# A state-space vision network on one core: a depthwise 13 x 13 convolution that takes 16 channels at a time and does its 13th kernel column as sixteen 32x32 products

## The chip, the cores and the metric

The kernel runs on one core of one Trainium2 chip. The metric is device time in microseconds: the median of three runs before the change is 6902.47 us (6889.23 to 6907.38). The profile is one further execution.

The engines are named as the profile names them: PE is TensorE's matmul side and PEld its weight loads, DVE is VectorE, ACT is ScalarE, POOL is GpSimd, SP is SyncE, which here only issues DMAs. ACT and POOL issue DMAs as well; an issued DMA then runs on 16 DMA engines that all queues share.

## What is computed

Eight images of 384 channels and 32 x 32 points go through four layers: two state-space blocks (the second with an attention gate and an MLP), a sum of seven depthwise convolutions with batch norms, and a pointwise convolution followed by a depthwise one with GELU. The change concerns the last two. Cut to what matters:

```python
def _L2_conv_ref(x, w_lk, w_b0, ..., bn_gamma, bn_beta, bn_mean, bn_var):
    dilates = (1, 1, 2, 3, 4, 5)
    out = bn_eval(dwconv(x, w_lk, 1), bn_gamma[0], ...)          # 13 x 13
    for i, (w, r) in enumerate(zip(branch_ws, dilates)):         # 5, 7, 7, 3, 3, 3
        out = out + bn_eval(dwconv(x, w, r), bn_gamma[i + 1], ...)
    return out

def _L3_conv_ref(x, pw_w, ..., dwk_w, ..., dw1_w, ...):
    x_pw = bn(einsum('bchw,oc->bohw', x, pw_w), ...) + x
    out = bn(dwconv(x_pw, dwk_w), ...)                           # 13 x 13
    out = out + bn(x_pw * dw1_w.reshape(1, -1, 1, 1), ...)
    return gelu(out, approximate=False)
```

All the branches of one layer together are one depthwise convolution with a 13 x 13 kernel per channel, and that is how the kernel does them. All arithmetic is in float32.

## The kernel before

**Order.** `network` first runs `layers`, the two state-space blocks and the MLP, up to about 6347 us of the span. There the order of each engine's instructions is written out by hand: a `Plan` has numbered slots, and every step is put into one. Then come `Depthwise.run` on `x3` (called run 1 here), `Pointwise.run`, and `Depthwise.run` on `x5` (run 2). These three have no order written by hand; the framework puts the instructions of each engine in a queue, and each queue runs in order.

**The kernel tables.** `prepare` is a generator whose pieces are put into consecutive slots near the beginning, from slot -50 on. It folds the batch norms, and for each of the two convolutions (`k2`, `k3`) and each of three chunks of 128 channels it loads the branch kernels (line 190, POOL's queue, seven loads for `k2` and one for `k3`), sums them on DVE into one 13 x 13 kernel (198 or 202 and 204), zeroes a row buffer of 1024 values (206), copies the kernel into it in four pieces (210), and stores it to `k_rows` in DRAM with one DMA from POOL's queue (212), 4096 contiguous bytes for each partition. In the table the 13 columns of a kernel stand as 4 steps `j` (`KP = 4`) by 4 shifts `s`, column 4 j + s, so three of the sixteen places are empty; the 13 rows stand in a strip of `HK = 64` rows of zeros. A small pair of steps before it (140, 145) writes 384 biases out in 4-byte pieces and reads them back.

**The depthwise step.** One step `g` of 48 takes 8 channels, as two sets `a` of four channels `q`. A channel's images stand in `xp` with 32 image rows on 32 partitions, and four copies of them, shifted by 0, 1, 2 and 3 columns, stand in the four groups of 32 partitions. Two DMAs from POOL's queue load the images (`images`, line 984), one for the first and one for the second set, and four DVE copies make the shifts (999 to 1001): two of 32 partitions by 1212 values, two of 64 by 1208. `kernels` (970) loads the tables into `wt`: a band matrix for each column, made by reading the strip of zeros at 32 offsets, 512 contiguous bytes per partition and channel, in four DMAs of 128 KB, three from SP's queue and one from ACT's. `early` loads the first ten steps' tables ahead, from POOL's queue, while `layers` is still at its last MLPs.

A product (1008) has 128 rows of contraction, 32 output rows of one channel and 256 columns (8 images x 32). For one set it runs over `j` and then over the four `q`, which lie in different groups of 32 output columns of the array. The set's 128 x 256 outputs fill one PSUM tile; ACT adds the bias, with GELU in run 2 (1013), and issues the store (1014). The store of run 1 has 1024 contiguous bytes for each partition, that of run 2 eight pieces of 128 bytes.

**Buffers.** `xps` has 4, `wts` 11, `o` 4, and the PSUM pool 4 tiles of one bank. A `past` tile of 16100 values per partition and one of four PSUM banks lie ahead of the convolution's buffers: there are the buffers that `layers` uses to its end (`fh`, `rows_out`, the PSUM tiles `mm` and `f`), and what lies behind can be filled earlier. `Pointwise` has its buffers behind those of the convolution, and shares its PSUM pool.

Of the kernel before, what the change touches and what calls it, by code (L numbers as in the profile page):

```python
# [17 lines left out]
B = 8  # L18
# [20 lines left out]
PAST = 16100  # L39
# [27 lines left out]
class Plan:  # L67
# [3 lines left out]
    def __init__(self):  # L71
        self.slots = {}
# [4 lines left out]
    def run(self, slot):  # L77
        for fs in self.slots.pop(slot, ()):
            for f in fs:
                f()  # L80
# [30 lines left out]
def prepare(nc, k, vec, a, dram, tile, mm, got):  # L111
# [69 lines left out]
    for name in ("k2", "k3"):  # L181
        got[name] = dram.tile([C, 4, HK, KP], F32, name=f"{name}_rows")
        for c in range(KC):
            room, used[0] = tile("fh"), 0
# [20 lines left out]
            rows = tile("hc").rearrange("p q t -> p (q t)")[:, 0 : 4 * HK * KP]  # L205
            nc.vector.memset(rows, 0.0)
            rows = rows.rearrange("p (s r j) -> p s r j", s=4, j=KP)
            for s in range(4):
                n = (KS - s + 3) // 4
                nc.vector.tensor_copy(rows[:, s, low : low + KS, 0:n], t[:, s::4].rearrange("p j r -> p r j"))  # L210
            yield
            nc.gpsimd.dma_start(got[name][c * P : (c + 1) * P], rows)
# [730 lines left out]
class Depthwise:  # L943

    N2 = NG // 2
    NB, AHEAD = 4, 3
    NK, EARLY = 11, 10

    def __init__(self, tc, st):
        nc = self.nc = tc.nc
        self.keep = st.enter_context(tc.tile_pool(name="d_keep", bufs=1, reuse_waits="tile"))
        self.work = st.enter_context(tc.tile_pool(name="d_work", bufs=4, reuse_waits="tile"))
        self.psum = st.enter_context(tc.tile_pool(name="d_ps", bufs=4, space=PSUM, reuse_waits="tile"))
        self.wts = [self.keep.tile([P, 8, HW, KP], F32, name=f"wt{i}") for i in range(self.NK)]  # L960
        self.xps = [self.keep.tile([P, 8, B * WIDE + 2 * PAD], F32, name=f"xp{i}") for i in range(self.NB)]
        for t in self.xps:
            nc.gpsimd.memset(t, 0.0)

    def kernels(self, g, table, queues):
        wt = self.wts[g % self.NK]
        for s, queue in enumerate(queues):
            at = table.offset + (32 * g + s) * HK * KP
            windows = bass.AP(table.tensor, at, [[KP, HW], [4 * HK * KP, 8], [1, HW * KP]])
            queue.dma_start(wt[HW * s : HW * (s + 1)].rearrange("p q r j -> p q (r j)"), windows)  # L970
# [14 lines left out]

    def run(self, src, table, bias, func, store):
        nc = self.nc
        n = B * WIDE
        for g in range(self.AHEAD):
            self.images(g, src)  # L990
        for g in range(self.N2):
            wt, xp = self.wts[g % self.NK], self.xps[g % self.NB]
            if g + self.AHEAD < self.N2:
                self.images(g + self.AHEAD, src)
            if g + self.EARLY < self.N2:
                self.kernels(g + self.EARLY, table, (nc.sync, nc.scalar, nc.sync, nc.sync))
            for h in range(2):
                low, q = 2 * HW * h, slice(4 * h, 4 * h + 4)
                nc.vector.tensor_copy(xp[low + HW : low + 2 * HW, q, 0 : n - 1], xp[low : low + HW, q, 1:n])
            nc.vector.tensor_copy(xp[2 * HW :, 0:4, 0 : n - 2], xp[: 2 * HW, 0:4, 2:n])  # L1000
            nc.vector.tensor_copy(xp[: 2 * HW, 4:8, 2:n], xp[2 * HW :, 4:8, 0 : n - 2])
            for a in range(2):
                ps = self.psum.tile([P, T], F32, tag="ps", name="ps")
                for j in range(KP):
                    x = xp[:, :, 4 * j : 4 * j + n].rearrange("p q (b c) -> p q b c", c=WIDE)
                    for q in range(4):
                        c = 4 * a + q
                        nc.tensor.matmul(  # L1008
                            ps[HW * q : HW * (q + 1), : B * HW], wt[:, c, :, j], x[:, c, :, 0:HW],
                            start=j == 0, stop=j == KP - 1,  # L1010
                        )
                o = self.work.tile([P, B, HW], F32, tag="o", name="o")
                nc.scalar.activation(o, ps[:, : B * HW], func, bias=bias[:, 2 * g + a : 2 * g + a + 1])  # L1013
                nc.scalar.dma_start(store(2 * g + a), o)


class Pointwise:
# [4 lines left out]
    def __init__(self, tc, st, psum, w):  # L1022
        nc = self.nc = tc.nc
        keep = st.enter_context(tc.tile_pool(name="q_w", bufs=1, reuse_waits="tile"))
        self.work = st.enter_context(tc.tile_pool(name="q_work", bufs=3, reuse_waits="tile"))
        self.psum = psum
# [31 lines left out]
def network(ctx: ExitStack, tc: tile.TileContext, a: dict, out: bass.AP):  # L1058
# [36 lines left out]
    with ExitStack() as st:  # L1095

        past = st.enter_context(tc.tile_pool(name="past", bufs=1, reuse_waits="tile"))
        past.tile([P, PAST], F32, name="past")
        past_ps = st.enter_context(tc.tile_pool(name="past_ps", bufs=1, space=PSUM, reuse_waits="tile"))
        past_ps.tile([P, 4 * T], F32, name="past_ps")  # L1100
# [3 lines left out]
        point = Pointwise(tc, st, conv.psum, a["pw"])  # L1104
# [121 lines left out]
```

## Time and profile before

| What | us |
|---|---|
| Median of three runs | 6902.47 |
| Profiled execution: span from the first to the last instruction | 6870.5 |
| First matmul of run 1 | 6349.3 |
| First matmul of run 2 | 6671.5 |
| PE busy in the span | 5851.1 |
| DVE busy | 5755.9 |
| POOL busy | 5285.7 |
| ACT busy | 4475.3 |
| DVE copies of line 999, 192 of them | 153.6 |
| DVE copies of lines 1000 and 1001, 192 of them | 152.8 |
| ACT activations of line 1013, 192 of them | 91.0 |

The span is that of the profiled execution, and the difference to the median is what lies around it. A matmul of the program in float32 shows as two instructions. Busy time of a pipelined PE counts an instruction from its start to its modelled end, so four that overlap are counted once. The DMA share of a stretch can be over 1, as packets of several queues overlap on an engine.

This is the DMA view of the tables, images and stores (output and input, queue, number, size of each, median us to landing):

```profile
wt<-k_rows SPq DMA_DIRECT2D x228, 128.0 KB
xp<-x POOLq DMA_DIRECT2D x96, 152.0 KB, 5.1
xp<-x POOLq DMA_DIRECT2D x96, 151.0 KB, 5.2
x<-o ACTq DMA_DIRECT2D x96, 128.0 KB
out_dram<-o ACTq DMA_DIRECT2D x96, 128.0 KB
wt<-k_rows POOLq DMA_DIRECT2D x80, 128.0 KB, 5.9
wt<-k_rows ACTq DMA_DIRECT2D x76, 128.0 KB
k_rows<-hc POOLq DMA_DIRECT2D x6, 512.0 KB, 3.0
```

### The profile page before, as it was taken

Reading aid. Unit: us, or ns where it says so; the run is one execution under the profiler, and the core shown is the slowest. Engines: PE = TensorE matmul, PEld = TensorE weight load, DVE = VectorE, ACT = ScalarE, POOL = GpSimd, SP = SyncE. Lnnn points to the kernel's source line nnn. Section 1 sums busy time; section 2 is a strip of 40 time slices with the busy share of each in tenths; the row PEclk is TensorE's granted clock in tenths of the full one; section 3 lists DMA queues with packets and bytes.
Section 4 is the critical chain, followed back from the end, with each engine's and each line's share of the span. In section 5 each row is a group of like instructions: output and inputs, shape, how many; then the busy total and the mean of one; then the engine's idle time right before and its main releaser. Section 6 shows DMA issues by size and latency. Waiting matters only on the chain. (4 is left out here: it accounts for less than half of the span.)

```text
span 6870.5 us, 76836 instructions
## 1 busy us (share of the span) xinstructions
PE 5851.1 (85%) x22562; PEld 2082.8 (30%) x22562; DVE 5755.9 (84%) x4598; ACT 4475.3 (65%) x7478; POOL 5285.7 (77%) x2858
## 2 busy tenths in 40 slices
PE   6787787888988888888888888888898888978988
PEld 2222222222322232222222232223232222323745
DVE  3899999899888888889889898888888898791837
ACT  4777666767676776867676767767676667653222
POOL 3889888888888888888898888888888788772412
PEclk7789988999999999999999999999999989989999
DMA  4565555665656666666756566666675655754979
GB/s 130 162 175 158 154 158 151 162 182 159 182 155 165 169 170 163 161 168 170 176 157 179 161 175 165 167 165 169 161 172 160 165 162 162 173 132 123 287 213 236
DMA packets 944578, 1160.04 MB, mean 169 GB/s; under 512 B 301264, under 2 KB 537344, under 8 KB 944160
## 3 DMA queue, kind: packets, MB, share of 16 engines
q1 hardware_dynamic: 782080, 1059.11, 59.0%
q10 hardware_dynamic: 146928, 51.02, 3.1%
q0 software_dynamic: 15152, 44.99, 2.3%
q8 instruction: 183, 3.00, 0.2%
q14 instruction: 235, 1.93, 0.1%
HBM read 904.67 MB, written 199.49 MB: 161 GB/s over the span
## 5 line engine op out<-in xcount | busy, mean ns | idle before, releaser
L532 POOL TENSOR_TENSOR dbu<-B,ru 128x1024 f32<-128x1024 f32 x1536 | 3583.2, 2357 | 168.7 <-DMA B<-bc 92.3
L525 ACT ACTIVATE h<-rd,A 128x512 f32<-128x512 f32 x3072 | 2117.4, 691 | 887.4 <-DVE hc L561 521.2
L553 DVE TENSOR_TENSOR_SCAN h<-h,state,dbu 128x512 f32<-128x512 f32 x1152 | 1482.5, 1287 | 210.5 <-ACT h L525 74.6
L561 DVE TENSOR_TENSOR hc<-h,C 128x1024 f32<-128x1024 f32 x1152 | 1411.0, 1225 | 139.8 <-DMA C<-bc 22.2
L556 DVE TENSOR_TENSOR_SCAN h<-h,dbu 128x1024 f32<-128x1024 f32 x576 | 1317.9, 2288 | 221.0 <-ACT h L525 149.9
L572 POOL TENSOR_TENSOR hc<-dbu,C 128x1024 f32<-128x1024 f32 x384 | 903.1, 2352 | 702.1 <-DVE dbu L556 358.5
L583 PE MATMUL acc<-hc,fold 128*32 128x512 f32 x6144 | 1158.0, 662 | 321.6 <-DVE hc L561 239.9
L415 PE MATMUL mm<-xt,wi 128*128 128x512 f32 x2232 | 1116.9, 638 | 57.2 <-ACT delta L491 18.9
L703 PE MATMUL f<-mx,wi 128*128 128x512 f32 x1116 | 589.0, 635 | 141.7 <-ACT fh L707 99.9
L415 PEld LDWEIGHTS mm<-xt,wi 128*128 128x128 f32 x2232 | 419.9, 201 | 754.5 <-issue 435.5
L604 PE MATMUL mm<-u,wo 128*128 128x512 f32 x1152 | 589.9, 653 | 63.4 <-DMA wo<-in_l_out_dram 51.6
L716 PE MATMUL f<-fh,wo 128*128 128x512 f32 x1128 | 573.1, 625 | 73.2 <-DMA wo<-in_fc_dram 64.1
L583 PEld LDWEIGHTS acc<-hc,fold 128*32 128x32 f32 x6144 | 164.6, 112 | 1132.3 <-DVE hc L561 513.3
L553 DVE TENSOR_TENSOR_SCAN dbu<-h,state,dbu 128x512 f32<-128x512 f32 x384 | 470.5, 1267 | 15.8 <-ACT h L525 8.0
L556 DVE TENSOR_TENSOR_SCAN dbu<-h,dbu 128x1024 f32<-128x1024 f32 x192 | 438.1, 2282 | 48.1 <-ACT h L525 47.3
L439 PE MATMUL mm<-xp,taps 128*64 128x512 f32 x1536 | 408.7, 654 | 21.2 <-ACT state L569 8.1
L984 POOL DMA_DIRECT2D xp<-x x192 | 124.3, 648 | 382.1 <-PE ps L1008 182.7
L305 ACT ACT_TABLE_LOAD x289 | 370.8, 1283 | 5.9 <-PEq L1214 0.7
L1008 PE MATMUL ps<-xp,wt 128*32 128x256 f32 x6144 | 343.8, 381 | 34.7 <-ACT o L1013 21.1
L604 PEld LDWEIGHTS mm<-u,wo 128*128 128x128 f32 x1152 | 229.8, 208 | 427.1 <-issue 355.6
L580 PE MATMUL acc<-u,skip 128*128 128x512 f32 x384 | 226.1, 673 | 153.2 <-DVE u L588 150.6
L425 ACT ACTIVATE xp<-mm,b_in 64x512 f32<-64x512 f32 x384 | 261.6, 681 | 143.1 <-PE mm L415 140.3
(168 smaller groups left out, 5726.4 us busy)
## 6 DMA issues: line engine op xcount, KB each, us to landing
ru<-uu SPq DMA_DIRECT2D x1536, 128.0 KB
rd<-dd SPq DMA_DIRECT2D x1536, 128.0 KB
wi<-w_in SPq DMA_DIRECT2D x372, 192.0 KB
xp<-xp SPq DMA_DIRECT2D x384, 128.5 KB
dd<-delta SPq DMA_DIRECT2D x192, 256.0 KB
uu<-delta SPq DMA_DIRECT2D x192, 256.0 KB
wo<-in_l_out_dram SPq DMA_DIRECT2D x96, 384.0 KB
wi<-fc_w SPq DMA_DIRECT2D x192, 192.0 KB
```

The costliest lines, as they stand in the source:

```text
L415: nc.tensor.matmul(s.ps[m], w[:, c], s.xt[:, c], start=c == 0, stop=c == KC - 1)
L439: nc.tensor.matmul(s.ps[d][64 * h : 64 * h + 64], taps[:, h, j], xp[h][:, 2 * j : 2 * j + T], start=j == 0, stop=j == 1,)
L525: nc.scalar.activation(y[:, q], s.dr[d][1][h][:, q], AF.Exp, scale=s.layer.A[:, at : at + 1])
L532: nc.gpsimd.tensor_tensor(dbu, s.B[g].unsqueeze(1).to_broadcast([P, 2, T]), s.ur[d][1][h], ALU.mult)
L553: nc.vector.tensor_tensor_scan(to[:, q], y[:, q], dbu[:, q], first, ALU.mult, ALU.add)
L556: nc.vector.tensor_tensor_scan(flat_to, flat_y, flat_b, first, ALU.mult, ALU.add)
L561: nc.vector.tensor_tensor(hc, to, s.C[g].unsqueeze(1).to_broadcast([P, 2, T]), ALU.mult)
L572: nc.gpsimd.tensor_tensor(hc, y, s.C[g].unsqueeze(1).to_broadcast([P, 2, T]), ALU.mult)
L583: nc.tensor.matmul(s.acc[d][32 * r : 32 * r + 32], k["fold"], tiles[r // 2][:, r % 2], start=False, stop=n == PER - 2)
L604: nc.tensor.matmul(s.ps[m], w[:, d], s.us[d], start=d == 0, stop=d == KD - 1)
L703: nc.tensor.matmul(s.ps[m], s.w["in", m][:, c], s.xt[:, c], start=c == 0, stop=c == KC - 1)
L716: nc.tensor.matmul(s.down, s.w["out", 2 * m + f // KD][:, f % KD], s.hs[f], start=f == 0, stop=f == KF - 1)
```

## The change

- **Products.** A turn of the loop takes a pair of steps, 16 channels in four sets. Each set does three steps `j` as before. The 13th column of all four sets is done at the end of the pair, as sixteen products of 32 x 32: set `k` uses the partitions of shift `k` alone, at column offset 12 - k, and its four channels go to the four column groups, so that the sixteen products lie in sixteen different parts of the array.
- **Tables.** In DRAM the four channels of a quad now lie beside each other in each row, so that a partition's piece for four channels is 2048 contiguous bytes. `prepare` therefore writes them otherwise: a zeroed piece of 512 values is stored over the whole chunk with a repeated source (256 pieces of 2 KB), the kernel is copied in eight pieces instead of four, and four stores put the 13 rows into the strip, each with runs of `KP` values, 16 bytes, for 32 partitions x 4 shifts x 13 rows. The weights of a product are read 16 values apart instead of 4. The 13th column stands in the fourth place for every shift.
- **Copies.** The fourth copy of each step, 64 partitions by 1208 values, goes from DVE to ACT.
- **Buffers.** PSUM 8 tiles instead of 4, `xps` 6 instead of 4, images loaded 4 steps ahead instead of 3, tables 9 instead of 10. `past` shrinks to 3200 values, the four PSUM banks are no longer kept out, and the buffers of `Pointwise` move to the front, into the memory that `layers` uses to its end; they are filled at the same place of the program as before.

```diff
-PAST = 16100
+PAST = 3200
...
+            rows = tile("hc").rearrange("p q t -> p (q t)")
+            empty = rows[:, 0:T]
+            nc.vector.memset(empty, 0.0)
+            to = bass.AP(
+                got[name].tensor, got[name].offset + c * P * 4 * HK * KP, [[4 * HK * KP, P], [T, 4 * HK * KP // T], [1, T]]
+            )
+            nc.gpsimd.dma_start(to, empty.unsqueeze(1).to_broadcast([P, 4 * HK * KP // T, T]))
...
-            rows = tile("hc").rearrange("p q t -> p (q t)")[:, 0 : 4 * HK * KP]
-            nc.vector.memset(rows, 0.0)
-            rows = rows.rearrange("p (s r j) -> p s r j", s=4, j=KP)
+            rows = rows[:, T : T + 4 * KS * KP].rearrange("p (s r j) -> p s r j", s=4, j=KP)
             for s in range(4):
-                n = (KS - s + 3) // 4
-                nc.vector.tensor_copy(rows[:, s, low : low + KS, 0:n], t[:, s::4].rearrange("p j r -> p r j"))
+                nc.vector.tensor_copy(rows[:, s, :, 0 : KP - 1], t[:, s : KS - 1 : 4].rearrange("p j r -> p r j"))
+                nc.vector.tensor_copy(rows[:, s, :, KP - 1 :], t[:, KS - 1 :].rearrange("p j r -> p r j"))
             yield
-            nc.gpsimd.dma_start(got[name][c * P : (c + 1) * P], rows)
+            for q in range(4):
+                nc.gpsimd.dma_start(got[name][c * HW : (c + 1) * HW, :, low : low + KS, q], rows[q::4])
             yield
...
-    NB, AHEAD = 4, 3
-    NK, EARLY = 11, 10
+    NB, AHEAD = 6, 4
+    NK, EARLY = 11, 9
...
-            at = table.offset + (32 * g + s) * HK * KP
-            windows = bass.AP(table.tensor, at, [[KP, HW], [4 * HK * KP, 8], [1, HW * KP]])
+            at = table.offset + (8 * g + s) * HK * step
+            windows = bass.AP(table.tensor, at, [[step, HW], [4 * HK * step, 2], [1, HW * step]])
...
+        for pair in range(0, self.N2, 2):
+            sets = [(g, a) for g in (pair, pair + 1) for a in range(2)]
...
+            self.shifts(pair)
+            self.shifts(pair + 1)
+            tops = []
+            for g, a in sets:
                 ps = self.psum.tile([P, T], F32, tag="ps", name="ps")
+                tops.append(ps)
+                wt = self.wts[g % self.NK]
+                for j in range(KP - 1):
+                    x = columns(g, 0, P, 4 * j)
                     for q in range(4):
                         nc.tensor.matmul(
+                            ps[HW * q : HW * (q + 1), : B * HW], wt[:, a, :, q, j], x[:, 4 * a + q, :, 0:HW],
+                            start=j == 0, stop=False,
                         )
+            for k, (g, a) in enumerate(sets):
+                low, high = HW * k, HW * (k + 1)
+                x, wt = columns(g, low, high, KS - 1 - k), self.wts[g % self.NK]
+                for q in range(4):
+                    nc.tensor.matmul(
+                        tops[k][HW * q : HW * (q + 1), : B * HW], wt[low:high, a, :, q, KP - 1],
+                        x[:, 4 * a + q, :, 0:HW], start=False, stop=True, tile_position=(low, HW * q),
+                    )
+            for (g, a), ps in zip(sets, tops):
                 o = self.work.tile([P, B, HW], F32, tag="o", name="o")
                 nc.scalar.activation(o, ps[:, : B * HW], func, bias=bias[:, 2 * g + a : 2 * g + a + 1])
                 nc.scalar.dma_start(store(2 * g + a), o)
```

`shifts` holds the copies; the first three are DVE's, as before, and the last is

```python
        nc.scalar.copy(xp[: 2 * HW, 4:8, 2:n], xp[2 * HW :, 4:8, 0 : n - 2])
```

## The prediction

> **What bounds the kernel now.** I read the page's span, then busy time by stage (windows), then the depthwise lines by source, then engine timelines. The depthwise lines run in two stretches, called run 1 (on x3) and run 2 (on x5); their first and last matmuls start 170.0 and 194.5 us apart. Columns of the windows: stretch, us, busy us (instructions) of PE, PEld, DVE, ACT, POOL, PE clock, DMA share, GB/s. The second block is the source view of the matmul line.
>
> ```profile
> span 6870.5 us, 76836 instructions
> ```
> ```profile
> 6349.30:6519.80 170.50, 167.75 (x3072) 125.78 (x3072) 153.63 (x190) 44.53 (x94) 65.07 (x103) 1.00 1.04 282
> 6671.50:6870.50 199.00, 176.03 (x3072) 118.52 (x3072) 149.57 (x190) 45.48 (x96) 60.86 (x90) 0.99 1.08 234
> ```
> ```profile
> L1008 PE MATMUL ps<-xp,wt x6144: 377/378/643, 6349.3 to 6866.0; 128*32 128x256 f32 x199
> ```
>
> Each matmul of the code is two instructions, so 3072 per run; four to different output columns overlap. In run 1 most stretches of 256 take 13.62 to 13.64 us, 53.3 ns each; 3072 x 53.3 = 163.9, so run 1 is **bound by TensorE** (96%), DVE 90% busy. Run 2 has the same work and takes 24.5 us more: DMA share above 1, and ScalarE's queue is held up by issuing DMAs:
>
> ```profile
> 6701.98 2.87 ACTq L970 DMA_DIRECT2D wt<-k_rows  x1
> 6704.95 0.41 ACTq L1014 DMA_DIRECT2D out_dram<-o  x1
> 6705.46 0.47 ACT L1013 ACTIVATE o<-ps,b 128x256 f32<-128x256 f32 x1 [3.08 <-PE ps L1008]
> ```
>
> The timeline's columns are start, length, instruction, idle before and releaser: a table load sits 2.87 us in the queue, and the store and next activation come behind it. The output store writes 128-byte pieces, 1024 per DMA. Run 2 is **bound by the DMA engines, through ScalarE's queue**.
>
> A third place is the **beginning**, where the tables are made. ScalarE delivers the first step sizes `delta` at 93.4, but GpSimd multiplies them only behind the last table store:
>
> ```profile
> 92.81 0.60 ACT L491 ACTIVATE delta<-mm 128x512 f32<-128x512 f32 x1
> ...
> 46.81 1.71 POOL L140 DMA_DIRECT2D b_flat<-fh  x2 [6.65 <-DVE fh L186]
> ...
> 103.99 0.54 POOL L212 DMA_DIRECT2D k_rows<-hc  x1 [5.12 <-DVE hc L210]
> 104.55 1.27 POOL L495 TENSOR_TENSOR delta<-delta,u 128x512 f32<-128x512 f32 x1
> ```
>
> The chain goes on from there (dd and uu stores, their repeated loads, first scan at 127.5). So `prepare`'s chain on GpSimd is on the path, about 1 us for 1 us, though it is far from the diff's main part.
>
> **Part 1: the tables in `prepare`.** Six chunks. Before: loads, DVE work, one store of 128 pieces of 4096 B (0.54 us on GpSimd). After: a zeroing store (256 pieces of 2 KB; nearest row the 256-piece `wt` load, 0.58) and four stores of 32 x 4 x 13 = 1664 pieces of 16 bytes. Nothing in the trace has 1664 pieces. GpSimd's issue lengths: 128 pieces 0.54 to 0.55, 256 pieces 0.58, 384 pieces 0.76 to 0.99 (`b_flat<-fh`, 4-byte pieces, the pair above is 1.71). Low bound: pieces cost nothing, 0.55. High bound: all above 256 cost as between 256 and 0.99, 3.2 ns each: 0.58 + 1408 x 0.0032 = 5.1. I take the nearest row, `b_flat<-fh`, mean 0.855 at 384 against 0.544 at 128, 1.2 ns a piece: 0.544 + 1536 x 0.0012 = **2.4 us**. Per chunk: +4 x 2.4, +0.58, DVE copies eight of about 0.12 for four of 0.13 (+0.45), old store -0.54, the 0.91 us memset now ahead of the loads: 9.2 us, six times **+55** (ends 11 and 120). The first scan waits behind it all, no other work hides it. The queue gives a GpSimd DMA the semaphore of the eighth before it, so a load can also wait for a scatter's landing; `b_flat` took 8.5 us to land, so with cheap issues up to 4 us at three places; at 2.4 us an issue it is covered. The tables are first read 6.1 ms later; the zeroing store lands before the loads behind it.
>
> The 4-byte store's 8.5 us stands against 3.0 for the 4 KB store. The Trainium skill, "DMA: Bandwidth & Descriptors", Specifications, says that transfers under 512 B make the engine read, modify and write, a rule against 16-byte scatters; no run here separates that. By it only landing grows, which nobody awaits, so the sum stays.
>
> **Part 2: TensorE.** Per pair (16 channels): before 4 x 4 x 4 x 2 = 128 instructions, 32 rounds of 213 ns = 6.83. After: 24 rounds, 5.12, and 32 instructions of 32x32. If the 16 run side by side, 2 rounds, 0.43; if only the four columns do, 8 rounds, 1.71. Column tiles start 1 to 33 ns apart, so issuing does not limit; I take 0.43. Changing the array's shape costs: fold to 128x128 starts 521 ns apart against 428 within a shape, 0.09, twice: 0.19. Weights are now read 64 bytes apart, not 16: loads took 137 ns at 16 and 112 in the contiguous fold; up to the round's 213 they hide under matmuls, so 0. Sum **5.74** a pair, 138 a run (ends 134, and 169 without overlap).
>
> The Trainium skill, "TensorEngine Tiling (Array Packing)", Key Properties, says that a change of mode drains the engine. The row above agrees in kind (93 ns); were the drain a whole instruction, 378 less 213, it would be 0.33 a pair, 3 us a run more.
>
> **Part 3: copies and ScalarE.** DVE goes from four copies of 0.785 per 8 channels to three: 4.7 a pair, no bound. ScalarE gets 64x1208. It has no such row; 128x512 from SBUF takes 0.619 and 256 to 512 elements 0.474 to 0.675, 0.79 ns each; 8x1024 takes 1.148. Between 1.17 and 1.34: 1.25. Its order on the queue: an activation and its store repeat every 0.93 (run 1) or 1.03 (run 2). Behind a copy stand activations and stores, and for their banks TensorE waits; eight banks let one pair be read while the next is made. Run 1 a pair: 4 x 0.93 + 2 x 1.25 + two table issues of 0.33, half under the copies, and 0.1 of waits: **6.6**, so ScalarE becomes the bound: 158 for 170, **-12** (ends -32, TensorE's 138, and +3 at 7.2 with stores landing late in four `o` buffers).
>
> **Part 4: DMA and run 2.** By the trace's packet records (medians) 128 B take 13 ns of an engine, 512 B 27, 2048 B 84, an image packet of 4.8 KB 194. A pair before: four stores 3.33, eight table loads 3.46, images 1.55: 8.34 us of 16 engines. After, loads 2.69: 7.57. Loads go on for 39 of 48 steps: 19.5 pairs x 7.57, at the 94% that before reached (65 + 117 = 182 of 194.5): 157; then 4.5 pairs at ScalarE's 6.9: 31. Sum 188, **-7** (ends -17 at full use; +42 if ScalarE's queue, occupied some 8.05 a pair now, takes both copies, 2.5, on top).
>
> **Part 5: ends.** Four activations come together after a pair's last matmul, three more than before: 3 x 0.93 and 3 x 1.03, **+6**. Two more xp memsets (2 x 2.22) and 36 early loads for 40 lie on GpSimd between 6221 and 6330 beside the last MLPs: nothing; uncovered 4.4. The q_out memsets move into memory that the last down products hold until 6346.8; ahead of the image loads they would delay run 1 by up to 8. ScalarE's queue shows table issues between an activation and its store, not where the code has them, so order follows readiness: 0. On SP the load of `pw` now waits for `rows_out`'s last store, some us after 6347.6; behind it stand table loads for groups 9 and later, due about 30 us later: 0. The first four PSUM banks are the last MLP's; its last read ends at 6347.6, before the first matmul at 6349.3: 0.
>
> **Sum:** 55 - 12 - 7 + 6 = **+42**. The profiled run spans 6870.5, the median is 6902.5, 32 around it. 6912.5 in span, **6945** in time.
>
> **Rivals.**
> - *Cheap scatters* (0.55): prologue +11 to +23, rest as above: -2 to +10, **6906**. For it: 256 pieces cost only 0.04 more than 128. Against: 384 cost 0.2 to 0.4 more.
> - *The convolution goes to TensorE's pace, with cheap scatters*: 5.74 at the present 96% is 5.97, 143 in run 1 (-27), run 2 -17, ends +6, prologue +11: -27, **6875**, faster. It decides when copies hide beside waits of ScalarE's queue and an issue is below 1.7 us. For it: DMA issues overlap running activations in the timeline. Against: ScalarE's own sum, 6.3 at least.
> - *ScalarE's queue binds run 2*, copies on top of blocked issues: 55 - 12 + 42 + 6 = +91, **6993**.
> - *Scatters at the upper price*: 120 - 13 = +107, **7010**.
>
> **How the numbers follow.** Forecast 0.43, cheap scatters 0.20, TensorE's pace 0.15, ScalarE's queue 0.10, upper price 0.12. A measurement tells about 0.3%, 21 us. Slower: 0.39 of the forecast and the last two, 0.61; within: 0.04 + 0.16 + 0.03 = 0.23; faster 0.16. The range reaches 6885 to 7010; the forecast alone, with scatters from 1.7 to 3.4 us, 6928 to 6969.
>
> **What would show it.** Issue length of a scatter on GpSimd and the start of the first scan (127.5 now, 182 expected); first-to-last matmul of run 1 (158) and run 2 (188); ScalarE's copy (1.25); start spacing of the 32x32 instructions. Wrong: if the scatter issues take under 1.7 us, or the first scan moves by under 30.

## The result, and the profile after

The changed kernel takes **7116.16 us** (median of four runs, 7108.07 to 7122.36) where the kernel before takes 6900.36 (6889.23 to 6907.38): the ratio is 1.0315, 95% interval 1.03 to 1.0329. It is slower by 216 us; 42 were forecast.

The first lines are the page's span and two windows of the changed kernel, run 1 and run 2, in the columns of the windows before (stretch, us, busy us of PE, PEld, DVE, ACT, POOL, PE clock, DMA share, GB/s):

```profile
span 7114.5 us, 77011 instructions
...
6540.70:6727.00 186.30, 157.17 (x3072) 94.62 (x3072) 111.25 (x142) 96.33 (x141) 72.33 (x103) 0.97 0.98 265
6880.30:7114.00 233.70, 168.19 (x3072) 96.77 (x3072) 111.39 (x142) 99.45 (x145) 60.02 (x89) 0.86 0.93 199
```

TensorE is no longer busy all through, VectorE and ScalarE have slack, and yet both runs are longer and fewer bytes move in a second. The granted clock is 0.86 in run 2 (0.99 before), but in the median a round of four 128-row products follows the one before in 216 ns in both runs, so the products' own pace is not what lengthens run 2. No engine's busy time explains the runs; the waits do. These are the source views of the 128-row products, of ScalarE's copy and of VectorE's copies of 32 partitions, with what their engines idled for ahead of them (us, times) and, for ScalarE's copy, who waited for it:

```profile
L1024 PE MATMUL ps<-xp,wt x4608: 377/378/641, 6540.7 to 7106.9; 128*32 128x256 f32 x192
...
  ACT xp L994: 186.4, 44
```
```profile
L994 ACT COPY xp<-xp x96: 1190/1197/1203, 6541.5 to 7096.5; 64x1208 f32<-64x1208 f32 x96
...
  DVE xp L992: 80.1, 17
...
  PE ps L1024: 88.0, 20
  POOL xp L985: 28.6, 5
```
```profile
L992 DVE COPY xp<-xp x192: 776/783/893, 6539.0 to 7094.8; 32x1212 f32<-32x1212 f32 x192
...
  DMA xp<-x: 148.7, 84
```

A copy takes 1.197 us, near the 1.25 priced, but TensorE waits for it, because the copy itself waits in ScalarE's queue for VectorE's copies, and these for images.

The beginning changed most. First GpSimd's timeline (start, length, instruction, idle before and what ended it), then a line of SP's and one of ScalarE's, then the source view of the 24 table stores:

```profile
98.09 4.57 POOL L218 DMA_DIRECT2D k_rows<-hc  x4 [3.84 <-DVE hc L215]
102.64 0.72 POOL L190 DMA_DIRECT2D k_rows<-hc  x1
103.24 1.78 POOL L197 DMA_DIRECT2D fh<-in_dw_dram  x3
113.05 0.54 POOL L197 DMA_DIRECT2D fh<-in_dw_dram  x1 [8.02 <-DMA k_rows<-hc]
124.25 0.54 POOL L197 DMA_DIRECT2D fh<-in_dw_dram  x1 [10.67 <-DMA k_rows<-hc]
...
237.15 1.27 POOL L501 TENSOR_TENSOR delta<-delta,u 128x512 f32<-128x512 f32 x1
```
```profile
238.72 1.83 SPq L511 DMA_DIRECT2D dd<-delta  x2
```
```profile
269.11 1.28 ACT L497 ACT_TABLE_LOAD   x1 [148.92 <-DMA dd<-delta]
```
```profile
L218 POOL DMA_DIRECT2D k_rows<-hc x24: 1128/1140/1176, 68.5 to 236.0; - x24
...
DMA to landing us min/median/max: 8.2/21.1/35.3
```

A store of 1664 pieces of 16 bytes is issued in 1.14 us but lands 21.1 us later in the median (the 4 KB store before: 3.0). The next chunk's loads stand behind it on GpSimd's queue, and some wait for its landing before they are issued. The larger part is that loads which are issued at once land late too, and VectorE waits for them. The waits from 60 to 290 us (us in total, times, longest), then VectorE's from the kernel before:

```profile
DVE fh L209 <- DMA fh<-in_dwk_dram: 85.7, 3, 35.9
DVE fh L205 <- DMA fh<-in_dw_dram: 82.8, 4, 39.3
...
POOL fh L197 <- DMA k_rows<-hc: 47.2, 8, 10.7
```
```profile
DVE fh L198 <- DMA fh<-in_dw_dram: 26.5, 4, 16.2
...
DVE fh L202 <- DMA fh<-in_dwk_dram: 12.0, 3, 4.3
```

So the first `delta` multiplication starts at 237.15 instead of 104.55. Its `dd` store, issued by SP at 238.7, is waited for until 269: the 16 DMA engines are the same for every queue. From 98 to 141 us packets of GpSimd's queue keep them 88.5% busy while all queues together move 21 GB/s.

The spans by stretch, from the starts and ends of scans and matmuls. The third column is the kernel before with 8 output buffers `o` (the experiment e9 below), a second profile of the same layer part:

| stretch, us | before | e9 | after | after less before |
|---|---|---|---|---|
| to the first scan | 127.5 | 127.5 | 288.8 | +161.3 |
| first to last scan | 6052.5 | 6067.2 | 6071.3 | +18.8 |
| last scan to run 1 | 169.3 | 169.5 | 180.5 | +11.2 |
| run 1, first to last matmul | 170.0 | 172.4 | 185.4 | +15.3 |
| between | 152.1 | 149.4 | 154.3 | +2.1 |
| run 2 | 194.5 | 199.9 | 227.3 | +32.9 |
| tail | 4.6 | 4.9 | 6.9 | +2.3 |

The sum is +244, the spans' difference. The medians differ by 216, because the profiled execution of before was a quick one: e9's scans take 6067 for 6052.5 with the same instructions, as they do in the changed kernels (6063 to 6074 in most; 6080 and 6091 in e11 and e12). So nearly all of the **+19 in the scans** lies within what two profiles of the old layer part differ by; the beginning, the start of run 1 and the two runs are the change's.

### The profile page after: what moved, and what is told of

Read it like the earlier page. It is cut to its first block, busy times and chain, and to the rows that moved or that the text cites. A ratio compares the mean times of both kernels' runs of the same rounds, so it can differ in the third digit from the quotient of the medians.

```text
span 7114.5 us, 77011 instructions
## 1 busy us (share of the span) xinstructions
PE 5849.3 (82%) x22562; PEld 2035.6 (29%) x22562; DVE 5675.2 (80%) x4526; ACT 4581.6 (64%) x7574; POOL 5318.0 (75%) x2876
## 5 line engine op out<-in xcount | busy, mean ns | idle before, releaser
L562 DVE TENSOR_TENSOR_SCAN h<-h,dbu 128x1024 f32<-128x1024 f32 x576 | 1317.9, 2288 | 223.8 <-ACT h L531 157.0
L559 DVE TENSOR_TENSOR_SCAN dbu<-h,state,dbu 128x512 f32<-128x512 f32 x384 | 470.5, 1268 | 14.9 <-ACT h L531 12.1
L1024 PE MATMUL ps<-xp,wt 128*32 128x256 f32 x4608 | 284.5, 401 | 111.2 <-ACT xp L994 88.0
```

The lines of the kernel that those rows point to most:

```text
L559: nc.vector.tensor_tensor_scan(to[:, q], y[:, q], dbu[:, q], first, ALU.mult, ALU.add)
L562: nc.vector.tensor_tensor_scan(flat_to, flat_y, flat_b, first, ALU.mult, ALU.add)
```

## The experiments

Profiles of the same code differ by 3.5 us in run 1 and 5.6 in run 2 (after, e1 and e2: 185.4, 188.9, 186.4 and 227.3, 223.7, 229.3). A number beside a time is its ratio to the kernel before on the same chip, with the 95% interval.

### The beginning: pieces of 16 bytes

**e1_large_pieces**

```diff
-    nc.gpsimd.dma_start(got[name][c * HW : (c + 1) * HW, :, low : low + KS, q], rows[q::4])
+    flat = got[name][c * HW : (c + 1) * HW].rearrange("g s r q j -> g (s r q j)")
+    at = 2 * q * T
+    nc.gpsimd.dma_start(flat[:, at : at + 4 * KS * KP], rows[q::4].rearrange("p s r j -> p (s r j)"))
```

> The changed kernel, but each of the 24 table stores writes 32 pieces of 832 bytes instead of 1664 of 16: as many stores, of the same bytes, issued at the same places (the pieces land at other places of the table, so the two depthwise runs compute with a wrong kernel). Theory: the landing of 16-byte pieces costs the prologue its time. A store then lands in about 3 us instead of 7 to 14, the first scan starts at 130 to 150 instead of 288.8, and the time falls from 7116 by 140 to 160, to 6955 to 6975; the two runs stay at 185 and 227. Rival (issue on GpSimd): 1664 pieces took 1.15 us to issue against 0.54 for 128, so 24 x 0.6 = 15 us at most come back, 7101. Rival (the number of DMAs behind one another on the queue's semaphores): nothing comes back, 7116.

**e2_64_bytes** stores 13 pieces of 64 bytes a channel at every second table row.

> The changed kernel, but each table store writes 416 pieces of 64 bytes instead of 1664 of 16 (same bytes; they land at other places of the table, so the depthwise runs use a wrong kernel). Theory with a price by the piece: a store takes a quarter of its time to land beyond the fixed part of about 2 to 3 us, so 3.5 to 5.5 us, and the first scan starts at 165 to 190. With a price by the byte: as in the changed kernel, 289. With a threshold between 16 and 64 bytes: as with 832-byte pieces, 130 to 150.

Measured: 6957.92 us (ratio 1.0089, 1.0061 to 1.0118) and 6971.46 (1.0104, 1.0066 to 1.0142, two executions). The first scan starts at 134.2 and 138.9. The source views of the stores, e1, then e2:

```profile
L220 POOL DMA_DIRECT2D k_rows<-hc x24: 520/528/536, 67.1 to 111.2; - x24
...
DMA to landing us min/median/max: 1.7/1.7/5.5
```
```profile
L219 POOL DMA_DIRECT2D k_rows<-hc x24: 649/660/687, 67.8 to 115.8; - x24
...
DMA to landing us min/median/max: 2.0/2.0/5.5
```

As many stores of the same bytes land in 1.7 and 2.0 us instead of 21.1, and nobody waits for them. The zeroing stores of 2 KB pieces behind them land in 3.2 us (20.8 in the changed kernel), and `dd`, issued at 113.3 in e1, is waited for until 115.4. Of the 161.3 us, 154.6 thus come from the 16-byte pieces, all but some 15 of them from landing: the issue lengths (1.14, 0.66, 0.53) give 24 x 0.6 = 15 us, the rival. A price by the piece falls too: a quarter of the pieces took not a quarter but almost nothing of the landing. Whether the size of 16 bytes or the number of pieces makes the step was not separated, nor whether it matters that the four stores of a chunk fall into the same 64 bytes of the table.

### The runs: copies, queues, buffers

**e3_copy_on_dve**

```diff
-        nc.scalar.copy(xp[: 2 * HW, 4:8, 2:n], xp[2 * HW :, 4:8, 0 : n - 2])
+        nc.vector.tensor_copy(xp[: 2 * HW, 4:8, 2:n], xp[2 * HW :, 4:8, 0 : n - 2])
```

> The changed kernel with the fourth row copy back on VectorE. Theory: ScalarE's queue (activations, 1.2 us copies, stores, table issues, all in order) sets the pace of both runs, so without the copies run 1 goes from 185 to 160-172 (VectorE then has 6.3 us a pair, 151 in all) and run 2 from 227 to 195-212; the time falls by 30 to 45, to 7070-7085. Rival (stores landing late on four output buffers, and DMA traffic): the copies were covered, run 1 stays within 5 us of 185 and run 2 within 5 of 227, the time within 10 of 7116. Rival (VectorE as the new bound because of its wait for image loads): slower, run 1 over 190.

Measured: 7082.70 (1.0267, 1.0243 to 1.0292); run 1 175.4, run 2 203.8. The first theory holds in the time; run 1 falls by 10 only, to just above its range. ScalarE now waits for something else, seen in the waits of its activations in run 1 (us in total, times, longest; 46.9 us of the second line lie ahead of the run's first activation):

```profile
ACT o L1038 <- DMA x<-o: 73.4, 33, 5.5
ACT o L1038 <- PE ps L1032: 65.8, 6, 46.9
```

**e4_tables_on_sp**: `(nc.sync, nc.scalar, nc.sync, nc.sync)` becomes four times `nc.sync`.

> The changed kernel with all four table loads of a group issued by SP, none by ScalarE. Theory (ScalarE's queue is held up by table issues that block 2 to 3 us each behind the output stores): run 2 falls from 227 by up to 39 x 1.0 = 25 to 35 us, to 192-205, run 1 from 185 to 175-180; the time falls by 25 to 40. Rival (the DMA engines' own time for stores and images): run 2 falls by less than 8, the time by less than 12. Run 1 should show the smaller part under either.

Measured: 7127.63 (1.0332, 1.0309 to 1.0355); run 1 218.8, run 2 220.8. A miss for the theory: run 1 is 33 us longer, and run 2 falls by 6.5, as the rival had it. SP's queue shows why:

```profile
SPq L971 <- DMA x<-o: 116.5, 43, 7.2
```

A table load on SP's queue now stands 116.5 us waiting for output stores to land, 7.2 at the longest (40.1 us in the changed kernel, 60.5 before); with a fourth load in that queue the tables come late. A table load needs nothing of an output store; why it waits for one is told behind e6. Taking ScalarE's issues away is no cure.

**e5_dve_o12** and **e6_o12**: the pool of `o` with `bufs=12` for 4, with the copy on VectorE and on ScalarE.

> The changed kernel with the fourth row copy on VectorE (as in e3_copy_on_dve) and 12 output buffers `o` for 4. In e3_copy_on_dve ScalarE's activations waited 73 us in run 1 and 100 us in run 2 for a store to land (`x<-o`, `out_dram<-o`): four stores leave in a burst after each pair and hold all four buffers. Theory (buffers and burst): these waits go, run 1 falls from 175 to 156-165 (VectorE's eight copies, 6.3 us a pair, are then the bound) and run 2 from 204 to 186-196; the time falls from 7083 to 7055-7068. Rival (the DMA engines cannot land the stores faster whatever the buffers): run 1 within 4 us of 175, run 2 within 4 of 204, the time above 7075.

> The changed kernel with 12 output buffers `o` for 4, the fourth row copy still on ScalarE. Theory (two separate costs: copies that wait in ScalarE's in-order queue, and late stores): the stores' part alone goes, run 1 from 185 to 172-182, run 2 from 227 to 208-220, the time from 7116 to 7087-7105. Rival (the buffers alone make the queue late, and the copies fit once they are there): as e5_dve_o12 or better, run 1 150-165. Rival (the copies alone): within 8 us of 7116.

Measured: 7074.61 (1.0251, 1.0237 to 1.0264), runs 176.7 and 207.3; and 7115.54 (1.031, 1.0295 to 1.0325), runs 187.0 and 220.4. Buffers bring next to nothing, with the copy or without it; the rivals hold, e5's time being 0.4 us under its mark. The view still has 68 us of activations waiting for stores in run 1 of e5.

The instruction records of the traces show what these waits are. The DMAs of SP and ScalarE share eight semaphores (248 DMAs in run 1 of e5, 31 on each), and a queue issues a DMA only when the one that had its semaphore last, mostly the eighth before it, has landed. ScalarE's queue stands 75 us of that run in such waits, 40 ahead of output stores and 35 ahead of table loads, and 1.4 us ahead of activations; the view puts them down to the activation that comes next. So the buffers of `o` were hardly waited for, and not in e3 either (61 us ahead of DMAs, 10 ahead of activations). In e4 SP's queue stands 131 us of run 1 in the same waits.

**e7_tables_o12_half** mends the tables. A channel's rows go out contiguously and come back with a quad on a partition:

```diff
+    nc.gpsimd.dma_start(flat[c * P : (c + 1) * P], rows.rearrange("p s r j -> p (s r j)"))
...
+    nc.gpsimd.dma_start(a4, got[name, "flat"].rearrange("(g q) n -> g (q n)", q=4))
...
+    nc.vector.tensor_copy(
+        b4.rearrange("g (s r q j) -> g q s r j", s=4, r=KS, q=4), a4.rearrange("g (q s r j) -> g q s r j", q=4, s=4, r=KS)
+    )
...
+    nc.gpsimd.dma_start(
+        got[name][:, :, low : low + KS].rearrange("g s r q j -> g s (r q j)"), b4.rearrange("g (s n) -> g s n", s=4)
+    )
```

> The changed kernel with four of its costs mended: the tables go contiguously (832 bytes a channel) to a second DRAM tensor, come back with a quad on a partition, are permuted by one VectorE copy per table and leave in pieces of 832 bytes; 12 output buffers; the fourth row copy on ScalarE for one group of a pair only; the zeroing of `q_out` behind run 1. Theory: first scan at 130-142 (289), from the last scan to the first matmul 168-173 (180), run 1 152-165 (185), run 2 184-200 (227); 7116 - 152 - 10 - 26 - 35 = 6893, between 6875 and 6912. Rival (something in the changed layout of pairs costs time by itself, beyond these four): above 6920.

Measured: 6945.07 (1.007, 1.0055 to 1.0085): first scan 137.2, 175.2 to run 1, runs 179.4 and 222.3. The beginning comes back as expected, and 5 us at the start of run 1. The runs miss the ends of their ranges by 14 and 22: something in the new structure costs time beyond the four.

**e9_before_o8** is the kernel before with `bufs=8`.

> The kernel before with 8 output buffers `o` for 4. TensorE was 96% busy in its run 1, so that stays at 170; its activations waited 13 us in run 2 for stores, so run 2 goes from 194.5 to 186-195: 6893-6903. It is also a second profile of the old layer part: from first to last scan it took 6052 us before and 6066 to 6071 in the four profiles of changed kernels. If the change makes these 14 to 19 us, it is 6052 again here; if a profile of the old kernel differs so by chance, it is 6060 or more.

Measured: 6895.64 (0.9995, 0.9985 to 1.0005), run 1 172.4, scans 6067.2: the reading by chance, as in the table above. Run 2, 199.9, did not shorten, against what was expected.

### The runs: DMA engines and how a pair ends

**e8_full_rows** starts from e5 and drops the 32x32 products:

```diff
-                for j in range(KP - 1):
+                for j in range(KP):
...
-                            start=j == 0, stop=False,
+                            start=j == 0, stop=j == KP - 1,
...
-            for k, (g, a) in enumerate(sets):
...
-                        x[:, 4 * a + q, :, 0:HW], start=False, stop=True, tile_position=(low, HW * q),
```

> e5_dve_o12 with the 13th column taken in a fourth step of 128 rows, as in the kernel before, and no 32x32 products (the last step multiplies rows that belong to other columns, so the convolution's sum is another). TensorE then needs 6.83 us a pair again instead of 6.05. Theory (the DMA engines are the wall in both runs: their share was 1.01 and 1.03 of e5_dve_o12's runs): run 1 moves from 176.7 to at most 182, run 2 stays within 5 of 207; the time within 12 of 7075. Rival (TensorE's pace still decides): 24 x 0.78 = 19 us more in each run, 7110.

**e10_half_tables** is e5 with the table of only one of a group's two quads loaded from group 11 on.

> e5_dve_o12, but from group 11 on only the first of a group's two quads has its table loaded (32 pieces of 2 KB for 64; the second quad multiplies by a table left from an earlier group). Theory (DMA wall): the engines' time falls by 37 of 48 groups x 0.64 MB... in packets, 37 x 128 x 122 ns / 16 = 36 us a run; run 1 goes from 176.7 to the next limit, VectorE's 12.6 us for two pairs, 157-164, and run 2 from 207 to 172-185; the time from 7075 to 7030-7045. Rival (the store landings and ScalarE's queue by themselves, whatever the traffic): both runs within 6 us.

**e11_old_tables** and **e12_old_tables_nk15** keep pairs, 32x32 products and banks, with the tables, their store and their loads of before; e12 has `NK, EARLY = 15, 13` for `11, 9`.

> The changed kernel with the tables laid out and loaded as before (a channel's rows together, loads in 512-byte pieces, one contiguous 4 KB store a channel in the beginning), the fourth copy on VectorE, the zeroing of `q_out` behind run 1; the pairs, the 32x32 products and eight banks stay. Theory: first scan at 128-132, from the last scan to the first matmul 170-173; runs as with 2 KB pieces in e3_copy_on_dve and e5_dve_o12, 170-180 and 200-210, since a table's packets took 133 us of an engine per MB-like unit before and 122 after, 8% apart; the time 6905-6925. Rival (2 KB packets themselves slow the other queues): run 1 at 158-168, run 2 at 185-195, 6885-6900. Rival (2 KB pieces save what they should): runs 15 us longer each, 6940 or more.

> e11_old_tables with 15 table buffers for 11 and 13 groups loaded ahead of each run for 9, in the memory that the change's layout left free. Theory (DMA wall): four groups of 39 fewer in the run, each 1.25 us of 16 engines, so 4 to 6 us less in each run than in e11_old_tables, 8 to 12 in the time. Rival: no difference beyond 4 us.

Measured: e8 7056.83 (1.0224, 1.0209 to 1.024), e10 7017.18 (1.0168, 1.0153 to 1.0184), e11 6964.73 (1.0093, 1.0078 to 1.0108), e12 6967.73 (1.0089, 1.0072 to 1.0105). The windows of e5, e8 and e10, run 1 and run 2 each:

```profile
6533.90:6710.60 176.70, 155.54 (x3071) 97.56 (x3072) 148.82 (x190) 39.01 (x92) 77.29 (x99) 0.97 1.01 275
6861.70:7069.10 207.40, 169.09 (x3072) 99.88 (x3072) 148.88 (x190) 40.16 (x93) 68.70 (x90) 0.89 1.03 220
```
```profile
6540.40:6708.40 168.00, 167.74 (x3072) 123.40 (x3072) 155.66 (x190) 45.13 (x95) 61.42 (x100) 0.99 1.03 289
6863.50:7052.80 189.30, 173.57 (x3072) 121.33 (x3072) 152.38 (x190) 45.11 (x95) 59.44 (x90) 0.99 1.09 245
```
```profile
6530.80:6691.20 160.40, 154.76 (x3072) 100.68 (x3072) 148.74 (x190) 41.08 (x92) 81.95 (x98) 0.99 0.89 247
6840.30:7004.70 164.40, 153.04 (x3072) 96.34 (x3072) 148.89 (x190) 42.34 (x93) 74.24 (x90) 0.99 1.00 221
```

e10 shows that the table bytes set the runs: with fewer of them they fall by 16 and 43 us, the second by more than expected. It does not tell through what: the 16 engines may be full, or the eight semaphores come free sooner when each DMA is shorter, for the number of DMAs is the same. A run with the same bytes in fewer DMAs was not made. e8 is the surprise: with **more** TensorE work the runs are 9 and 18 us shorter, and the same engines move 289 GB/s for 275. Neither of its expectations had that. e11 against e3, which differ in the tables (and in where `q_out` is zeroed): 193.8 and 223.8 for 175.4 and 203.8, so the 2 KB pieces do save some 18 to 20 us a run in this structure, and the prediction's part about them stands (the first expectation of e11 falls, the last holds). e12's four groups ahead shorten the runs by 3.5, which is no more than profiles differ by, and 11.7, but the time not at all.

**e13_bunched** is e8 with the last step of all four sets behind the first three steps of all four; **e14_small_first** is e5 with the 32x32 products first (the second cut):

```diff
+            tops = [self.psum.tile([P, T], F32, tag="ps", name="ps") for _ in sets]
+            for steps in (range(KP - 1), range(KP - 1, KP)):
+                for (g, a), ps in zip(sets, tops):
+                    wt = self.wts[g % self.NK]
+                    for j in steps:
```
```diff
+                        x[:, 4 * a + q, :, 0:HW], start=True, stop=False, tile_position=(low, HW * q),
...
-                            start=j == 0, stop=False,
+                            start=False, stop=j == KP - 2,
...
-                        x[:, 4 * a + q, :, 0:HW], start=False, stop=True, tile_position=(low, HW * q),
```

> e8_full_rows (no 32x32 products, a fourth step of 128 rows instead, so another sum), with the fourth step of all four sets of a pair behind the first three steps of all four: the same work on every engine, but the four accumulations end within 1.7 us of one another. Theory (bunched ends cost the runs their time): run 1 goes from 168 to 175-185, run 2 from 189 to 200-212, the time from 7057 to 7075-7090. Rival (the 32x32 products themselves, by their change of shape): as e8_full_rows, within 4 us in each run, 7057.

> e5_dve_o12 with the sixteen 32x32 products ahead of the twelve-column steps of their pair instead of behind them: the same instructions, but the four accumulations end 1.3 us apart, one after the other. Theory (bunched ends): run 1 from 176.7 to 157-168, run 2 from 207 to 180-190, the time from 7075 to 7035-7050. Rival (the 32x32 products themselves): within 4 us of e5_dve_o12 in each run.

Measured: e13 7058.68 (1.0247, 1.0232 to 1.0263), runs 182.4 and 200.5; e14 7045.54 (1.0228, 1.0214 to 1.0242), runs 180.6 and 194.8. What the activations of run 1 waited for, e8 and then e13, and e13's windows:

```profile
ACT o L1030 <- DMA x<-o: 2.6, 3, 0.9
```
```profile
ACT o L1029 <- DMA x<-o: 68.2, 32, 4.4
```
```profile
6516.00:6698.40 182.40, 173.96 (x3069) 125.47 (x3072) 148.89 (x190) 41.57 (x93) 76.63 (x103) 0.96 0.97 269
6850.10:7050.60 200.50, 177.46 (x3072) 119.27 (x3072) 149.11 (x190) 40.98 (x93) 66.45 (x90) 0.96 1.02 230
```

The same instructions with their ends bunched lengthen the runs by 14.4 and 11.2 us, without any 32x32 product, and the activations' idle time that ends with a store's landing grows from 2.6 to 68.2 us. The whole time did not grow with them, 7058.7 for 7056.8: in e13's profile the first scan starts at 271.7, in e8's at 286.2, with the same code there, on another chip; so the verdict rests on the two stretches. A table of time per four groups, from the starts of matmuls (the run's twelfths), shows the rest:

| run 1 | us for each four groups |
|---|---|
| before | 13.8 13.8 13.8 13.8 14.9 14.3 13.8 14.9 15.0 13.8 14.3 13.6 |
| after | 19.6 12.1 20.2 12.1 12.1 22.8 14.4 12.1 13.8 22.2 12.1 11.8 |
| e5 | 14.0 13.0 14.0 13.0 16.2 15.4 14.5 16.6 15.3 14.5 16.6 13.6 |
| e8 | 15.8 13.8 13.8 13.8 13.8 13.8 13.8 13.8 13.8 13.8 13.8 14.1 |
| e13 | 15.4 13.8 13.8 13.8 13.8 13.8 14.7 15.3 18.3 16.6 19.5 13.6 |
| e14 | 20.5 16.6 15.1 12.4 12.4 12.4 12.8 15.3 16.2 14.7 16.2 15.8 |

The 12.1 of the changed kernel is TensorE's new pace (6.05 us a pair). It is reached, and lost again. e14 misses its expectation in both runs. In run 1 its first three entries lose 11.2 us on e5, probably because the first small products need the copies of two groups, and most later ones are back at 15 to 16. In run 2 it gains 12.5, 4.8 less than the range asked. That its time lies in its range is luck: its first scan came 13.8 us earlier than e5's, with the same code there.

**e17_small_first_act** puts the ScalarE copy into e14 (with 12 `o`).

> e14_small_first with the fourth row copy on ScalarE. Theory (the copy costs by itself: it waits in ScalarE's in-order queue for VectorE's copies, which wait for images, with activations and stores behind it): run 1 180.6 to 186-200, run 2 194.8 to 205-225, the time from 7046 to 7060-7095. Rival (it costs only beside bunched ends): both runs within 4 us of e14_small_first or faster, as VectorE has 1.6 us a pair less to do.

Measured: 7103.82 (1.0293, 1.0278 to 1.0309), above the range, of which 11.8 are a later first scan; runs 185.9 and 223.1. So the copy costs by itself, 28 us in run 2 (and 5 in run 1, little more than profiles differ by). In run 2 TensorE, VectorE and GpSimd wait in a ring:

```profile
PE ps L1021 <- ACT xp L994: 45.0, 7, 8.2
```
```profile
DVE xp L992 <- DMA xp<-x: 90.8, 45, 10.5
```
```profile
POOL xp L985 <- ACT xp L994: 67.9, 9, 11.9
```

GpSimd's next image load waits until the copy has read its buffer, the image lands late, VectorE's copy and then ScalarE's come late. In e14 VectorE waited 33.7 us for images there.

### Can it be made faster than before?

**e15_mended**: e14 with e7's tables (zeroed by one store each), late `q_out`, 15 table buffers. **e16_full_rows_mended**: the same with e8's order, zeros in the table's empty places, and the permuting put among the first scans. **e18_tables_late**: the permuting behind the layers, on GpSimd (and 5 `o` for 6). The remarks behind `#` name the run:

```diff
-            put(AT["prepare"][0] + j * AT["prepare"][1] // 4, next, steps)
+            put(AT["prepare"][0] + j * AT["prepare"][1] // 4 if j < 26 else 6 * j - 116, next, steps)   # e16
...
+            nc.gpsimd.tensor_copy(t[:, 1].rearrange(...)[:, q], t[:, 0].rearrange(...)[:, q])            # e18
```

> The change with every cost found so far mended: tables permuted through a second DRAM tensor and stored in 832-byte pieces, zeroed by one store a table; four row copies on VectorE; 32x32 products first in a pair; zeroing of `q_out` behind run 1; 15 table buffers and 13 groups loaded ahead; 6 output buffers. Theory: first scan 130-137, scans 6066-6075, then 170-175, run 1 153-166, between 150-160, run 2 172-186, tail 5: 6870-6890, faster than the kernel before (6900) by 0.1 to 0.5%. Rival (if bunching is not the cause): runs as e5_dve_o12, 177 and 200, and 6910 or more.

> e15_mended without the 32x32 products: the 13th column in a fourth step of 128 rows (the table holds zeros there for the three other column shifts), each set ending by itself as before; the permuting of the tables through the second DRAM tensor moved behind the first scans. Theory: first scan 128-133, scans 6066-6075, 168-173 to the first matmul, run 1 164-168 (TensorE at 13.8 us for two pairs), 150-155, run 2 182-190, tail 4.5: a span of 6865-6890, a time of 6870-6892, faster than the kernel before by 0.1 to 0.5%. Rival (the layer part takes on what the beginning loses, or the runs are at the DMA wall whatever is done): within 0.1% of the kernel before.

> e16_full_rows_mended with the permuting of the tables moved behind the layers and from VectorE to GpSimd, which idles there for 46 us before the table loads. Theory: first scan 120-128, the first 96 scans 288-291 again (308 in e16_full_rows_mended), scans 6066-6075, 170-180 to the first matmul, run 1 166-172, 150-155, run 2 180-188: a span of 6865-6890, a time of 6870-6890, 0.1 to 0.4% faster than before. Rival (the layers' first scans need the same time from a start that is earlier, whatever was moved there): the scans grow by what the beginning wins, and the time is within 0.1% of the kernel before.

Measured: 6902.93 (1.0018, 1.0006 to 1.0029), 6906.16 (1.0004, 0.9994 to 1.0013), 6904.39 (1.0012, 1.0003 to 1.0021). No version beats the kernel before. Run 2 is shorter in all three (191.4, 182.1, 180.6), and each loses it elsewhere: e15 begins at 139.2 and has run 1 at 175.5; e16's scans take 6107.6, the first 96 of them 307.8 for 289; in e18 run 1 takes 193.4, as most image loads stood behind 52 table loads on GpSimd, and TensorE waited 23 us after its first set:

```profile
PE ps L1026 <- DVE xp L996: 23.2, 1, 23.2
```

Loading the images first there was not tried.

## Why the prediction was wrong

The direction was right, the size was not: +216 lies outside the range, whose upper end held one dear case at a time. Of the marks named ahead, the issue length (1.14 us) is under the 1.7 that would make the prediction wrong, and the first scan moved by 161 where 55 was expected.

**The step that failed first** is in part 1: "By it only landing grows, which nobody awaits, so the sum stays", with "at 2.4 us an issue it is covered". Issue was 1.14 us, below the estimate, and e1 and e2 show that the pieces of 16 bytes cost 154.6 us, at most 15 of it in issue and the rest in landing. The wait had been seen (a load waits for an earlier store's landing on GpSimd's queue), but with `b_flat`'s landing of 8.5 us, a store of 384 pieces, and for three places. The table stores land 21.1 us late, the branch kernels' loads behind them land late with them (VectorE waits 168.5 us for these, 38.5 before), and their traffic holds up `dd` on another queue as well (ScalarE's idling of 148.92 us ends with it). In place of +55 stands +161; the rival with dear issues had 120 for a wrong reason.

The Trainium skill, "DMA: Bandwidth & Descriptors", Specifications, says that below 512 bytes an engine reads, modifies and writes. No run shows that itself. The 21.1 us at 16 bytes would fit such a rule; the 2.0 at 64 bytes, against 1.7 at 832, show no price of it, and here the measurement decides.

**Part 2** and the copy's price were near: a pair takes 6.05 us where 5.74 was estimated, and 96 copies take 1.197 us each where 1.25 was. One reading was off by a step: the stretches of 13.62 to 13.64 us hold 255 steps from start to start and not 256, which take 13.8; TensorE's floor in run 1 was 165.8 and not 163.9. TensorE's time fell as reckoned and was worth nothing.

**Part 3** failed at "Run 1 a pair: ... 6.6, so ScalarE becomes the bound": a sum of what stands on ScalarE's queue, with 0.1 us for waits. Run 1 took 185, not 158, at 96 us of ScalarE busy. The copy waits in order behind activations and stores and for VectorE, and GpSimd's image loads wait for it: 10 and 24 us (e3), 5 and 28 with ends spread (e17).

**Part 4**: the table loads' saving was real (e11 against e3), but it was priced by medians: by the packet records of run 2 a 2 KB packet took 123 ns in the mean where 84 was taken, and the loads kept the 16 engines busy for 72.9 us where 81.8 stood before, 9 us less and not 15. And the run was reckoned from work that comes evenly. For run 1 before, "bound by TensorE" was only part of it: its DMA share was 1.04, and SP's queue stood 110.5 us of it waiting for DMAs to land.

**Part 5** counted four bunched ends once a run, +6 for both. They recur in every pair: four stores and the release of two groups' images come together, 14 and 11 us (e13). How these become time is argued: in e13 the engines moved 269 GB/s in run 1 where they moved 289 in e8, so they were not at their limit, and four stores at once take four of the eight semaphores; no run separates the two. So run 1 goes, by steps: 170.0 before, 168.0 with 2 KB pieces and full rows (e8), 176.7 with the 32x32 products behind the pair (e5), 185.4 with ScalarE's copies (and 4 `o`; 187.0 with 12, e6); run 2: 194.5, 189.2, 207.3, 227.3 (220.4). The zeroing of `q_out`, set at 0 after a delay of up to 8 had been named, did stand ahead of the image loads, and the first row copy came 9.6 us after the last `rows_out` piece (0.5 in e15, with the zeroing behind run 1); of the 11 us e15 got 8 back.

## What to carry to other kernels

Price a small-piece DMA by its landing as well as its issue, and then ask which instruction behind it on its queue, and which transfer on any other queue, waits for that landing. Where the queues stand waiting for DMAs to land, as here at a DMA share near 1, moving work off the busiest engine wins nothing, and making several results end together loses: spread stores and buffer releases. Where a view says that an activation waits for a store, look at whether it is the activation or the next DMA of its queue that waits, before you add buffers. Before an operation goes to an idle in-order engine, look at what it waits for and who waits for it there, not at the engine's busy time.

## What was not expected of the hardware

Stores of 26.6 KB in 1664 pieces of 16 bytes land in 8.2 to 35.3 us, in 416 pieces of 64 bytes in 2.0 to 5.5. The medians, 21.1 and 2.0, are a step of ten for a factor of four in pieces; part of the 21.1 is that the stores queue behind one another: the first of a chunk's four lands in 8.2 to 14.7 us, the others in 13.6 to 35.3. And with DMA shares of 1.03 and 0.97, the same instructions moved 289 GB/s in run 1 when they came evenly (e8) and 269 when four sets ended together (e13).
